# Attention and a selective scan: the projection's distance from its scan, the place of a copy, and which products GpSimd takes

## The chip, the cores and the metric

The kernel runs on one core of a Trainium2 chip. The metric is device time in microseconds (us) for one execution, the median of several runs. A difference of about 0.2% is the least that a measurement of this kernel can tell from no change.

## The reference

The input x is an fp32 image batch of 2 x 256 x 256 x 128. Two layers follow each other, each with a residual and a group norm in front. Layer 0 is attention along one image axis. Layer 1 is a state space layer, and the change is in it alone. Cut to what matters:

```python
xz = x @ in_proj_w.T                      # 128 -> 512
xi, z = split(xz, 2)                      # 256 channels each
xi = silu(depthwise_conv3x3(xi))          # along h, w
dts, Bs, Cs = split(x_proj_w @ xs)        # 8, 16 and 16 rows
delta = softplus(dt_w @ dts + dt_b)       # 256 channels
h_t = exp(delta_t * A) * h_(t-1) + (delta_t * xs_t) * B_t   # state 256 x 16
y_t = sum_n h_t[:, n] * C_t[n] + Ds * xs_t
y = layer_norm(y) * silu(z)
out = x + y @ out_proj_w.T
```

The recurrence runs over all 65536 pixels of an image in order, for 256 channels times 16 states.

## The kernel before, in words

The first part (attention, to about 2.5 ms) is not touched. The second part works in 128 *steps*: 64 per image, each of R = 4 image rows, so T = 1024 pixels.

**Units and slots.** A step's recurrence has 256 x 16 = 4096 rows, that is NU = 32 *units* of 128 partitions (32 channels times 4 states). Units are numbered t = 32 k + i for step k. In order of i they run over halves h of the channels (16 units each), in a half over four groups m of states, and in a group over four quarters q of channels. One *slot* of the schedule belongs to each unit. Each compute engine executes in the order in which the loop at the end of the kernel writes it out by hand; only the DMA queue of SyncE is ordered by the framework's scheduler.

A unit passes through these pieces:

- `decay(t)` (L956, ScalarE): exp(delta * A) of a unit into a PSUM tile da. There are two such tiles, for even and odd units, so a decay follows the last reader of the unit two before it.
- `drive(t)` (L966, GpSimd): (delta * x) * B for a *pair* of units into the SBUF tile hb, one 128 x 2048 instruction. hb has three buffers. It reads du_r and bb.
- `scan(t)` (L978, VectorE): the recurrence along T with da, hb and the state kept from the step before. It overwrites da, or, for a *pooled* unit, its half of hb.
- the product with C: `product(t)` on VectorE (L992, 128 x 1024) or, for pooled pairs, `products(t)` on GpSimd (L1001, 128 x 2048, two slots later), into yc, which has four pair buffers. Pooled pairs start at 6, 14, 22, 26 and 30 of each step: ten of the 32 products. [...]
- `remember(t)` (L983, ScalarE): the last column of the scan into the state.
- `add_up(t)` (L1024, PE): adds four units' yc into y in PSUM, six slots after the group's first unit. `start_up` (L1015) begins y with Ds * xs. `y_out` (L1037, ScalarE) copies y to SBUF seven slots after the last group's first unit, so at slots 3 and 19 of a step.

**Loads.** `fetch(t)` runs six slots ahead and loads, through SyncE's queue alone, rows of B and C repeated over partitions (bb, cc; two buffers each, L928) and delta and delta * xs (delta_r, five buffers; du_r, three pair buffers; L942). These come from DRAM tiles that the projection of the step wrote.

**Projection.** `project(k)` lays the pieces that make a step's inputs into slots relative to `base`: the image rows are turned and normalised (base, base + 1), a 3 x 3 conv as nine PE matmuls in four groups (`conv`, `conv_out`), the gate z (`gate`, `gate_out`, `silu_z` at base + 28, L718), `silu_xs` at base + 36 (L695), the rows for B, C and dt (`states`, `size`), `softplus` at base + 52 (L763) and, on GpSimd, `times`, which makes delta * xs in two halves (base + 55 and 56, L773) and writes them to DRAM. Each Silu or Softplus sits between two table loads of ScalarE. All the PE pieces share one PSUM buffer.

**Output.** `finish_row` brings one image row to the output in nine slots, starting at slots 8, 16, 24 and 32 after the end of its step: turn (PE), statistics and norm (ScalarE, L840 to L852), turn back, `gated` (VectorE, yg, L871), `mix` (PE) and `leave`.

In each slot the order was: the drive two to three units ahead, a pooled pair's products, the decay of the next unit, the scan and product of this one, the copy of y, the pieces of projection and output, the sums on PE, and the state.

Of the kernel before, what the change touches and what calls it, by code (L numbers as in the profile page):

```python
# [10 lines left out]
ALU = mybir.AluOpType  # L11
# [10 lines left out]
def attn_then_ssm_kernel(  # L22
# [26 lines left out]
    nc = tc.nc  # L49
# [78 lines left out]
    NSG = NS // SR  # L128
# [149 lines left out]
    with ExitStack() as actx:  # L278
# [242 lines left out]
        end = B * NA  # L521
        BY = 6
        with tc.manual_schedule(engines=engines):
            load(0)
            for n in range(-1, end + 1):
# [22 lines left out]
                if new:  # L548
                    project(n + 1, "m0", "qT", wqk)
# [3 lines left out]
                if new:  # L553
                    project_out(n + 1, "qT", bqk)
                    project(n + 1, "m1", "v1", wv1)
                    project_out(n + 1, "v1", bv1_c)
# [30 lines left out]
    NU = NCG * NSG  # L587
    NM = NQ * NSG

    POOLED = (6, 14, 22, 26, 30)  # L590
    s1 = ctx.enter_context(tc.tile_pool(name="s1", bufs=1))
    s2 = ctx.enter_context(tc.tile_pool(name="s2", bufs=2))
    s3 = ctx.enter_context(tc.tile_pool(name="s3", bufs=3))
# [27 lines left out]
    def project(k):  # L621

        b, s = steps[k]
        rs, sh = gn1[b]
        base = k * NU - 72
        n = min(R, H - 1 - R * s)
        v = given[k] = {}
        o = {}
# [150 lines left out]
        for r in range(0, n, RB):  # L779
            t = base + r // RB  # L780
# [3 lines left out]
        for c in range(4):  # L784
            h, i = divmod(c, NB)
            t = base + c * CY + 3
# [125 lines left out]
    def unit(t):  # L912

        k, i = divmod(t, NU)
        h, i = divmod(i, NM)
        m, q = divmod(i, NQ)
        return k, h, m, q

    spreads, repeats = {}, {}

    def fetch(t):
        k, h, m, q = unit(t)
        v = given[k]
        if q == 0:

            for name, row in (("bb", m * SR), ("cc", NS + m * SR)):
                tl = repeats[name, k, h, m] = s2.tile([P, T], F32, name=name)
                nc.sync.dma_start(  # L928
                    out=tl, in_=v["bc"][row : row + SR, :].partition_broadcast(CQ)
                )  # L930
        if m == 0:

            for name in ("delta", "du"):
                if name == "delta":
                    tl = s5.tile([P, T], F32, name="delta_r")
                elif q % 2 == 0:
                    pair = spreads["pair", k, h, q] = s3.tile([P, 2, T], F32, name="du_r")
                    tl = pair[:, 0, :]
                else:
                    tl = spreads["pair", k, h, q - 1][:, 1, :]  # L940
                spreads[name, k, h, q] = tl
                nc.sync.dma_start(  # L942
                    out=tl,
                    in_=v[name][h, q * CQ : (q + 1) * CQ, :]
                    .unsqueeze(1)
                    .to_broadcast([CQ, SR, T]),
                )

    def pooled(t):
        return t % NU - t % 2 in POOLED  # L950

    def decay(t):
        k, h, m, q = unit(t)
        da = units[t]["da"] = ps_d.tile([P, T], F32, name=f"da{t % 2}")
        g = h * NQ + q
        nc.scalar.activation(  # L956
            da, spreads["delta", k, h, q], AF.Exp, scale=a_neg[:, g, m : m + 1]
        )

    def drive(t):  # L960

        k, h, m, q = unit(t)
        hb = s3.tile([P, 2, T], F32, name="hb")
        units[t] = {"pair": hb, "hb": hb[:, 0, :]}
        units[t + 1] = {"hb": hb[:, 1, :]}
        nc.gpsimd.tensor_tensor(  # L966
            hb,
            spreads["pair", k, h, q],
            repeats["bb", k, h, m].unsqueeze(1).to_broadcast([P, 2, T]),
            ALU.mult,  # L970
        )

    def scan(t):
        k, h, m, q = unit(t)
        u = units[t]
        st = states_of[steps[k][0]][:, h * NQ + q, m : m + 1]
        u["h"] = u["hb"] if pooled(t) else u["da"]
        nc.vector.tensor_tensor_scan(u["h"], u["da"], u["hb"], st, ALU.mult, ALU.add)  # L978

    def remember(t):  # L980
        k, h, m, q = unit(t)
        st = states_of[steps[k][0]][:, h * NQ + q, m : m + 1]
        nc.scalar.copy(st, units[t]["h"][:, T - 1 : T])  # L983

    def product(t):
        k, h, m, q = unit(t)
        u = units[t]
        if t % 2 == 0:
            yc = s4.tile([P, 2, T], F32, name="yc")
            for i in range(2):  # L990
                units[t + i]["yc"] = yc[:, i, :]
        nc.vector.tensor_tensor(u["yc"], u["h"], repeats["cc", k, h, m], ALU.mult)  # L992

    def products(t):

        k, h, m, q = unit(t)
        hb = units[t]["pair"]
        yc = s4.tile([P, 2, T], F32, name="yc")
        for i in range(2):
            units[t + i]["yc"] = yc[:, i, :]  # L1000
        nc.gpsimd.tensor_tensor(  # L1001
            yc, hb, repeats["cc", k, h, m].unsqueeze(1).to_broadcast([P, 2, T]), ALU.mult
        )
# [3 lines left out]
    def start_up(t):  # L1007

        k, h, _, _ = unit(t)
        xr = s1.tile([P, T], F32, name="xr")  # L1010
        nc.sync.dma_start(out=xr, in_=given[k]["xs"][h])
        y = outs["y"] = ps_y.tile([P, T], F32, name="y")
        for i in range(NB):
            cols = slice(i * TB, (i + 1) * TB)
            nc.tensor.matmul(y[:, cols], d_diag[:, h, :], xr[:, cols], start=True, stop=False)  # L1015

    def add_up(t):

        _, _, m, _ = unit(t)
        y = outs["y"]  # L1020
        for i in range(NB):
            cols = slice(i * TB, (i + 1) * TB)
            for q in range(NQ):
                nc.tensor.matmul(  # L1024
                    y[q * CQ : (q + 1) * CQ, cols],
                    sel,
                    units[t + q]["yc"][:, cols],
                    start=False,
                    stop=(m == NSG - 1),
                )  # L1030
        for q in range(NQ):
            del units[t + q]

    def y_out(t):
        k, h, _, _ = unit(t)
        ys[k, h] = s2.tile([P, T], F32, name=f"ys{h}")
        nc.scalar.copy(ys[k, h], outs["y"])  # L1037

    for k in range(len(steps)):
        project(k)  # L1040
        finish(k)
    end = len(steps) * NU
# [7 lines left out]
    with tc.manual_schedule(engines=engines):  # L1050
        for t in range(min(slots), max(slots) + 1):
            if 0 <= t + AHEAD < end:
                fetch(t + AHEAD)
            if 0 <= t < end and t % (NU * NSTEP) == 0:
                st = s1.tile([P, NCG, NSG], F32, name="state")
                nc.gpsimd.memset(st, 0.0)
                states_of[steps[t // NU][0]] = st
            if 0 <= t + 3 < end and t % 2:
                drive(t + 3)
            if 0 <= t - 2 < end and t % 2 == 0 and pooled(t - 2):  # L1060
                products(t - 2)
            if 0 <= t + 1 < end:
                decay(t + 1)
            if 0 <= t < end:
                scan(t)
                if not pooled(t):
                    product(t)
            if 0 <= t - 7 < end and unit(t - 7)[2:] == (NSG - 1, 0):
                y_out(t - 7)
            others, on_pe = slots.pop(t, ((), ()))  # L1070
            for piece, args in others:
                piece(*args)
            for piece, args in on_pe:
                piece(*args)
            if 0 <= t - 5 < end and (t - 5) % NM == 0:
                start_up(t - 5)
            if 0 <= t - 6 < end and (t - 6) % NQ == 0:
                add_up(t - 6)
            if 0 <= t < end:
                remember(t)  # L1080


# [35 lines left out]
```

## Time and profile before

| | |
|---|---|
| median of 3 runs | 16278.99 us (16275.81 to 16286.14) |
| span of the profiled execution | 16298.5 us |
| VectorE (DVE) busy | 14642.8 us, 90% |
| PE busy | 13879.5 us, 85% |
| GpSimd (POOL) busy | 13035.7 us, 80% |
| ScalarE (ACT) busy | 10842.9 us, 67% |
| DMA | 3452 MB, 212 GB/s on the mean |
| first scan of the steps | 2678.85 us |
| drives (L966) | 2048 of 4538 ns |
| scans (L978) | 4096 of about 2340 ns |
| products on VectorE (L992) | 2816 of 1225 ns |
| products of pairs on GpSimd (L1001) | 640 of 4545 ns |

The shares of the whole span mix the attention part with the steps. In a row of a group, the first number after the bar is busy time in us, the second the mean of one instruction in ns; after the second bar stands how long the engine was idle just before these instructions, and what ended most of that idle time. In the timeline each row begins with start and duration in us.

### The profile page before, as it was taken

Reading aid. Unit: us, or ns where it says so; the run is one execution under the profiler, and the core shown is the slowest. Engines: PE = TensorE matmul, PEld = TensorE weight load, DVE = VectorE, ACT = ScalarE, POOL = GpSimd, SP = SyncE. Lnnn points to the kernel's source line nnn. Section 1 sums busy time; section 2 is a strip of 40 time slices with the busy share of each in tenths; the row PEclk is TensorE's granted clock in tenths of the full one; section 3 lists DMA queues with packets and bytes.
Section 4 is the critical chain, followed back from the end, with each engine's and each line's share of the span. In section 5 each row is a group of like instructions: output and inputs, shape, how many; then the busy total and the mean of one; then the engine's idle time right before and its main releaser. Section 6 shows DMA issues by size and latency. Waiting matters only on the chain. (4 is left out here: it accounts for less than half of the span.)

```text
span 16298.5 us, 178168 instructions
## 1 busy us (share of the span) xinstructions
PE 13879.5 (85%) x59451; PEld 7046.9 (43%) x59451; DVE 14642.8 (90%) x12484; ACT 10842.9 (67%) x20003; POOL 13035.7 (80%) x3216
## 2 busy tenths in 40 slices
PE   6999997888888888888888888888888888888886
PEld 5877783333333333333333333333333333333333
DVE  7665555999999999999999999999999999999998
ACT  3555554667666666766666666666776676677665
POOL 0111114999999999999999999999999999999998
PEclk9999998999999999999999999999999999999998
DMA  4322223666666666666666666666666666666665
GB/s 183 132 92 78 94 78 135 236 233 237 237 230 233 237 233 236 239 232 235 232 237 232 232 229 234 236 234 234 238 234 233 234 237 233 236 239 232 234 232 180
DMA packets 1428907, 3452.13 MB, mean 212 GB/s; under 512 B 119784, under 2 KB 711184, under 8 KB 1407504
## 3 DMA queue, kind: packets, MB, share of 16 engines
q1 hardware_dynamic: 1427984, 3440.73, 61.0%
q8 instruction: 468, 7.67, 0.2%
q14 instruction: 455, 3.73, 0.1%
HBM read 2752.41 MB, written 687.88 MB: 211 GB/s over the span
## 5 line engine op out<-in xcount | busy, mean ns | idle before, releaser
L966 POOL TENSOR_TENSOR hb<-du_r,bb 128x2048 f32<-128x2048 f32 x2048 | 9237.6, 4538 | 354.3 <-DVE da L978 296.2
L978 DVE TENSOR_TENSOR_SCAN da<-da,state,hb 128x1024 f32<-128x1024 f32 x2816 | 6607.2, 2346 | 163.1 <-ACT da L956 160.2
L676 PE MATMUL u_ps<-xn,w_tap 128*128 128x512 f32 x9216 | 4481.8, 629 | 617.0 <-ACT state L983 607.5
L956 ACT ACTIVATE da<-delta_r,a_neg 128x1024 f32<-128x1024 f32 x4096 | 4588.5, 1120 | 91.8 <-ACT state L983 0.4
L992 DVE TENSOR_TENSOR yc<-da,cc 128x1024 f32<-128x1024 f32 x2816 | 3449.1, 1225 | 287.3 <-PE y L1024 113.8
L1001 POOL TENSOR_TENSOR yc<-hb,cc 128x2048 f32<-128x2048 f32 x640 | 2908.7, 4545 | 527.6 <-ACT state L983 493.0
L978 DVE TENSOR_TENSOR_SCAN hb<-da,state,hb 128x1024 f32<-128x1024 f32 x1280 | 2941.9, 2336 | 199.1 <-ACT state L983 166.4
L676 PEld LDWEIGHTS u_ps<-xn,w_tap 128*128 128x128 f32 x9216 | 1762.1, 201 | 3108.4 <-issue 2110.6
L1024 PE MATMUL y<-yc,sel 128*32 128x512 f32 x16384 | 2409.3, 712 | 16.6 <-POOL yc L1001 16.6
L435 POOL TENSOR_TENSOR x1g<-xc,bo_all 128x512 f32<-128x512 f32 x256 | 315.7, 1271 | 1844.3 <-DVE stats L484 1843.1
L983 ACT COPY state<-da 128x1 f32<-128x1 f32 x2816 | 458.2, 163 | 1266.7 <-DVE yc L992 1262.4
L828 PE MATMUL yt<-centre,ys 128*128 128x256 f32 x4096 | 1029.7, 395 | 250.2 <-ACT ob L889 250.2
L1024 PEld LDWEIGHTS y<-yc,sel 128*32 128x32 f32 x16384 | 477.4, 121 | 1743.3 <-issue 1518.6
L702 PE MATMUL z_ps<-xn,w_z 128*128 128x512 f32 x1024 | 691.8, 763 | 628.2 <-ACT sz L713 389.6
L385 ACT ACTIVATE e<-s_ps,nmx 128x256 f32<-128x256 f32 x1024 | 479.4, 478 | 967.9 <-DVE nmx L376 956.7
L983 ACT COPY state<-hb 128x1 f32<-128x1 f32 x1280 | 247.0, 193 | 1262.2 <-DVE hb L978 1262.2
L828 PEld LDWEIGHTS yt<-centre,ys 128*128 128x128 f32 x4096 | 741.3, 191 | 430.1 <-ACT ob L889 347.8
L744 PE MATMUL dt_ps<-xd,w_dt 8*128 8x512 f32 x1024 | 611.7, 678 | 345.2 <-ACT state L983 193.7
L889 ACT COPY ob<-o_ps 128x256 f32<-128x256 f32 x512 | 191.0, 373 | 948.6 <-PE o_ps L879 948.0
L879 PE MATMUL o_ps<-w_out,szr 128*128 128x128 f32 x4096 | 799.2, 277 | 0.0
L879 PE MATMUL o_ps<-w_out,yg 128*128 128x128 f32 x4096 | 797.9, 277 | 0.0
L352 DVE TENSOR_TENSOR v<-v_ps,bv_all 128x512 f32<-128x512 f32 x256 | 177.1, 692 | 594.5 <-PE v_ps L345 594.5
(133 smaller groups left out, 17404.3 us busy)
## 6 DMA issues: line engine op xcount, KB each, us to landing
bb<-bc_d SPq DMA_DIRECT2D x1024, 512.0 KB, 4.2
cc<-bc_d SPq DMA_DIRECT2D x1024, 512.0 KB, 4.8
delta_r<-delta_d SPq DMA_DIRECT2D x1024, 512.0 KB, 6.6
du_r<-du_d SPq DMA_DIRECT2D x1024, 512.0 KB, 5.5
sz_d<-sz SPq DMA_DIRECT2D x128, 1024.0 KB, 6.6
szr<-sz_d SPq DMA_DIRECT2D x512, 256.0 KB, 4.1
xs_d<-xs SPq DMA_DIRECT2D x128, 1024.0 KB, 9.0
xr<-xs_d SPq DMA_DIRECT2D x256, 512.0 KB, 5.7
```

Source lines behind the costliest of these rows:

```text
L676: nc.tensor.matmul(o["u"], w_tap[:, h, tap, :], xn[:, i * RB + dy : i * RB + dy + RB, dx : dx + W], start=(tap == 0), stop=(tap == 8),)
L702: nc.tensor.matmul(o["z"], w_z[:, h, :], xn[:, 1 + i * RB : 1 + (i + 1) * RB, 1 : W + 1], start=True, stop=True,)
L744: nc.tensor.matmul(o["dt"], w_dt[:, h, :], o["xd"][0:DR, i * TB : (i + 1) * TB], start=True, stop=True,)
L828: nc.tensor.matmul(o["yt"][:, j, :], ys[k, h][:, t0 + j * P : t0 + (j + 1) * P], centre[:, (1 - h) * P : (1 - h) * P + DI], start=(h == 0) ...
L879: nc.tensor.matmul(o["o"][:, j, :], o[by][:, h, j * P : (j + 1) * P], w_out[:, i, h, :], start=False, stop=(j == WT - 1 and h == NH - 1 an ...
L956: nc.scalar.activation(da, spreads["delta", k, h, q], AF.Exp, scale=a_neg[:, g, m : m + 1])
L966: nc.gpsimd.tensor_tensor(hb, spreads["pair", k, h, q], repeats["bb", k, h, m].unsqueeze(1).to_broadcast([P, 2, T]), ALU.mult,)
L978: nc.vector.tensor_tensor_scan(u["h"], u["da"], u["hb"], st, ALU.mult, ALU.add)
L983: nc.scalar.copy(st, units[t]["h"][:, T - 1 : T])
L992: nc.vector.tensor_tensor(u["yc"], u["h"], repeats["cc", k, h, m], ALU.mult)
L1001: nc.gpsimd.tensor_tensor(yc, hb, repeats["cc", k, h, m].unsqueeze(1).to_broadcast([P, 2, T]), ALU.mult)
L1024: nc.tensor.matmul(y[q * CQ : (q + 1) * CQ, cols], sel, units[t + q]["yc"][:, cols], start=False, stop=(m == NSG - 1),)
```

## The change

It has three parts. The projection of a step begins 64 slots, two whole steps, ahead of the step's first scan instead of 72, so each of its pieces moves by eight slots against the scans. The copy of y comes at the end of its slot, after the pieces and the state, so that ScalarE has done the slot's other work before it stands for the sums. And GpSimd takes eleven products of a step: the pair at 10 in place of the pair at 26, and one single product, that of unit 13, issued on GpSimd in the next slot before the decay.

```diff
-    POOLED = (6, 14, 22, 26, 30)
+    POOLED = (6, 10, 14, 22, 30)
+    SINGLE = 13
...
-        base = k * NU - 72
+        base = (k - 2) * NU
...
-        return t % NU - t % 2 in POOLED
+        return t % NU - t % 2 in POOLED or t % NU == SINGLE
...
-        nc.vector.tensor_tensor(u["yc"], u["h"], repeats["cc", k, h, m], ALU.mult)
+        eng = nc.gpsimd if pooled(t) else nc.vector
+        eng.tensor_tensor(u["yc"], u["h"], repeats["cc", k, h, m], ALU.mult)
...
             if 0 <= t - 2 < end and t % 2 == 0 and pooled(t - 2):
                 products(t - 2)
+            if 0 <= t - 1 < end and (t - 1) % NU == SINGLE:
+                product(t - 1)
...
-            if 0 <= t - 7 < end and unit(t - 7)[2:] == (NSG - 1, 0):
-                y_out(t - 7)
             others, on_pe = slots.pop(t, ((), ()))
...
             if 0 <= t < end:
                 remember(t)
+            if 0 <= t - 7 < end and unit(t - 7)[2:] == (NSG - 1, 0):
+                y_out(t - 7)
```

## The prediction, made before the changed kernel was run

> **What bounds the kernel now.** I read the page's busy shares first, then the busy time of each engine in the long stretch of steps (3000 to 16200 us), then the groups of that stretch by shape, and last the timeline of one step (the one whose first scan starts at 9031.5 us).
>
> ```profile
> 3000.00:16200.00 13200.00, 11117.48 (x44672) 4983.83 (x44670) 12694.85 (x7226) 9157.44 (x15911) 12372.31 (x2868) 0.93 0.68 234
> ```
>
> The columns are PE, PEld, DVE, ACT, POOL, then clock, DMA share, GB/s. VectorE is busy 96% of the stretch, GpSimd 94%; nothing else is close.
>
> ```profile
> L966 POOL TENSOR_TENSOR hb<-du_r,bb 128x2048 f32<-128x2048 f32 x1993 | 8989.4, 4538 | 317.6 <-DVE da L978 278.6
> L978 DVE TENSOR_TENSOR_SCAN da<-da,state,hb 128x1024 f32<-128x1024 f32 x2742 | 6433.6, 2346 | 28.5 <-ACT da L956 25.6 <-POOL state L1056 2.9
> ...
> L992 DVE TENSOR_TENSOR yc<-da,cc 128x1024 f32<-128x1024 f32 x2742 | 3358.4, 1225 | 278.8 <-PE y L1024 109.6 <-DVE da L978 2.7 <-issue 2.2
> L978 DVE TENSOR_TENSOR_SCAN hb<-da,state,hb 128x1024 f32<-128x1024 f32 x1244 | 2859.1, 2336 | 192.9 <-ACT state L983 160.9 <-ACT da L956 27.0
> L1001 POOL TENSOR_TENSOR yc<-hb,cc 128x2048 f32<-128x2048 f32 x623 | 2831.6, 4545 | 507.8 <-ACT state L983 480.2 <-issue 12.2 <-PE u_ps L676 8.8
> ...
> L773 POOL TENSOR_TENSOR xs<-delta,xs 128x1024 f32<-128x1024 f32 x248 | 587.4, 2369 | 0.0
> ```
>
> The last column is the one to read. No scan ever waits for a drive (L966): VectorE waits for ScalarE (its decays) and a little for PE. GpSimd waits for VectorE, so it runs ahead and has slack. From the first scan (2678.85) to the last (about 16239) 128 steps pass, so a step takes 105.9 us; that is the sum of VectorE's own work, about 103.0, and some 2.9 of waits.
>
> ```profile
> 9098.56 1.01 ACT L1037 COPY ys<-y 128x1024 f32<-128x1024 f32 x1 [2.11 <-PE y L1024]
> 9099.47 0.85 ACT L852 ACTIVATE yn<-yt,rstd 128x256 f32<-128x256 f32 x2
> ...
> 9100.89 1.12 ACT L956 ACTIVATE da<-delta_r,a_neg 128x1024 f32<-128x1024 f32 x1
> 9102.02 1.28 ACT L718 ACT_TABLE_LOAD   x1
> 9103.32 1.91 ACT L718 ACTIVATE sz<-sz 128x2048 f32<-128x2048 f32 x1
> 9105.25 1.28 ACT L619 ACT_TABLE_LOAD   x1
> ...
> 9106.73 1.12 ACT L956 ACTIVATE da<-delta_r,a_neg 128x1024 f32<-128x1024 f32 x1
> ...
> 9107.96 4.59 DVE L978 TENSOR_TENSOR_SCAN hb<-da,state,hb 128x1024 f32<-128x1024 f32 x2 [1.44 <-ACT state L983]
> ```
>
> This is where the largest of those waits is made. ScalarE stands 2.11 us at the copy of y, which is ahead of slot 19's other pieces; a Silu between two table loads follows, and scan 22, which comes early because no product of VectorE's stands before it, waits 1.44 us.
>
> **What the Trainium skill says.** "GPSIMD Engine Reference", section 3.1, gives 4497 ns for a GpSimd tensor_tensor on 2048 fp32 against 2293 ns on VectorE; this trace agrees (4538 and 4545 ns; VectorE 1225 ns at 1024). So a moved product takes about twice as long. "ScalarE: Activation LUTs", "What ACT_TABLE_LOAD costs", gives 1283 ns for a load and a drain on top; the load agrees, but no drain is seen between the lines above, so I count load, Silu, load as 4.5 us. "DMA: Bandwidth & Descriptors", "Anatomy of one DMA", says that a semaphore wait "happens on the issuing sequencer before dispatch". All loads here are issued by SyncE, so one waiting load holds all behind it; the trace agrees (SyncE issues nothing for up to 9 us, then several at once).
>
> **The change part by part.** Offsets come from the timeline: a scan with its product takes 3.58 us (even slots) or 3.52 (odd), a scan whose product is GpSimd's 2.25, each yg 0.60; on GpSimd a drive takes 4.49, a pair's product 4.55, a 1024 product 2.33 (from L773).
>
> *Eleven products instead of ten.* VectorE loses one product: 21 x 3.55 + 11 x 2.25 + 4 x 0.60 = 101.7 us a step (before: 22 and 10, 103.0). GpSimd gains 2.33: 16 x 4.49 + 5 x 4.55 + 3 x 2.33 = 101.6. Both engines now have the same work, so each wait of one for the other counts.
>
> *Copy of y at the end of its slot.* It removes no work. In slot 19 ScalarE no longer stands before the norm, the copy behind it and the state; the copy waits where scan 19's product is awaited anyway. At slot 3 it now stands in front of decay 5.
>
> *Projection 64 ahead.* All projection pieces move by 8 of 32 slots. As rows of the output recur every 8 slots, what shares a slot with them hardly changes: the three Silu and Softplus groups still stand two slots before a pooled pair (now slots 4, 20, 28). But delta x xs (L773) moves to slots 23 and 24, so the first du_r of the next step can be read only late in the step. In the built program SyncE's queue runs: write of du, delta_r 32, du_r 32, delta_r 33, cc, du_r 33, delta_r 34, du_r 34, write of sz, delta_r 35, du_r 35. delta_r 35 waits for the decay of scan 30 to free its buffer, which stands behind silu_z on ScalarE; queued behind it is du_r 35, and drive 34 waits for that. That is a new wait.
>
> Loop A, counted from scan 20: VectorE to the end of product 27, 3.58 + 4.12 + 4.50 + 14.20 = 26.4; decay 29 begins 0.25 later; from there to the end of decay 30 is 6.96 (9100.89 to 9107.85 above); delta_r is issued, 0.7; du_r is issued at 34.4 and lands L later. Then GpSimd without a pause from drive 34 to drive 20 of the next step: ten drives 44.9, four pairs' products 18.2, one single 2.33, together 65.4. Wakes 0.2. Sum: 100.0 + L. For L:
>
> ```profile
> delta_r<-delta_d SPq DMA_DIRECT2D x1024, 512.0 KB, 6.6
> du_r<-du_d SPq DMA_DIRECT2D x1024, 512.0 KB, 5.5
> ```
>
> (issues, size, median us to landing) and, of the tile du_r alone, the spread:
>
> ```profile
> DMA to landing us min/median/max: 3.3/5.5/9.2
> ```
>
> A du_r that is second in an otherwise quiet queue lands in 4.7 to 5.0 (the one of 9123.9 lands after 4.7); third or fourth in a train it takes 6.7. Here only sz (1 MB, issued 3 us earlier, 4.0 alone) and delta_r are ahead. I take 4.9: 104.9 us.
>
> Loop B, counted from the product of pair 6: GpSimd to the end of drive 28: nine drives 40.4, four pairs 18.2, three singles 7.0, together 65.6; scan 28 waits for that; VectorE from scan 28 to the end of scan 7: 12.2 + 26.5 = 38.7; wakes 0.3. In it ScalarE makes scan 6 wait: decay 5 begins 1.3 after scan 4 (state, copy of y), its Silu group ends decay 6 6.96 later, at 8.3, and scan 6 could begin at 7.7: 0.6. Sum: 105.2.
>
> The step is the longer loop, 105.2, and 0.1 for what the two do to each other: 105.3 against 105.9. That is 0.64 x 128 = 82 us less. PE's later start of a conv and the residue of ScalarE's work lie beside VectorE.
>
> *Start.* The first scan stood at its decay, which ScalarE reaches after the last conv, the turn of the third projection and silu_xs:
>
> ```profile
> 2678.85 2.36 DVE L978 TENSOR_TENSOR_SCAN da<-da,state,hb 128x1024 f32<-128x1024 f32 x1 [133.74 <-ACT da L956]
> ```
>
> With 8 slots fewer in front these come after it. The first drive (2658.7) then sets it: 2663.3, and the decay after silu_z at about the same time, so near 2665: 14 us less. The tail is untouched. 16279 - 82 - 14 = 16183 us.
>
> **The rivals.** *The late du_r (slower).* If the transfers bunch up and L is 6.7, loop A takes 106.7: 16279 + 0.8 x 128 - 14 = 16367. For it: the queue has three waits in a row, and landings go to 9.2. Against: the trains of today come from loads that all waited for one event. *VectorE sets it (faster still).* If GpSimd's waits fall into one another (L 4.4, no wait at scan 6), loops of 104.4 remain: 16279 - 192 - 14 = 16073. Against: both loops would have to be lucky. *No change.* GpSimd has no slack left, so waits of scans 16, 20 and 28 for drives take the place of waits for ScalarE: a step of 105.9, 16265. For it: idle GpSimd of 6.6 us a step today would have to fall below 4.3 for any gain.
>
> **How the numbers follow.** Forecast 0.50, late du_r 0.22, no change 0.15, VectorE alone 0.13. The range reaches from the fast rival to the slow one, 16065 to 16370. Of the forecast's half nearly all is faster by over 0.2% (below 16246), with the fast rival 0.62; within 0.2% 0.15; slower 0.23.
>
> **What would show it.** Right: a step of 105.3; scans 20 and 28 wait for POOL hb; drive 34 waits for the DMA of du_r for some 2 to 3 us; scan 22 no longer waits; a POOL group of 128 products of 1024 at about 2.37 us; the first scan near 2665. Wrong: waits of drives for du_r over 5 us a step (the late du_r), or no scan waiting for a drive (VectorE alone), or a new wait of decays on the copy of y.

## The result, and the profile after

The changed kernel takes 16677.32 us (median of 4 runs, 16672.46 to 16680.63) against 16278.85 us before: a ratio of 1.0244, 95% interval 1.0226 to 1.0262. It is 2.4% slower; 16183 us was forecast, and the range ended at 16370.

From the first scan to the last, 128 steps now take 13942.2 us, 108.95 each, where they took 105.96. That is 2.99 x 128 = 383 us more; the first scan comes 9 us earlier (2669.61 against 2678.85), the profiled spans differ by 372 (16670.4 against 16298.5, which is 20 above before's median), so all of the loss is in the steps.

The groups by shape of the changed kernel over the steps, 3000 to 16200 us (after the second bar: idle time just before these instructions, and who ended it):

```profile
L968 POOL TENSOR_TENSOR hb<-du_r,bb 128x2048 f32<-128x2048 f32 x1938 | 8766.6, 4549 | 889.4 <-DMA du_r<-du_d 702.6 <-DVE yc L995 79.2 <-DVE yg L873 54.3
L980 DVE TENSOR_TENSOR_SCAN da<-da,state,hb 128x1024 f32<-128x1024 f32 x2543 | 5971.8, 2348 | 818.3 <-POOL hb L968 779.3 <-ACT ys L1040 14.3 <-ACT da L958 12.8
...
L980 DVE TENSOR_TENSOR_SCAN hb<-da,state,hb 128x1024 f32<-128x1024 f32 x1331 | 3055.1, 2333 | 1.6 <-ACT state L985 1.6
L1004 POOL TENSOR_TENSOR yc<-hb,cc 128x2048 f32<-128x2048 f32 x606 | 2744.6, 4529 | 3.9 <-ACT state L985 3.9
...
L995 POOL TENSOR_TENSOR yc<-hb,cc 128x1024 f32<-128x1024 f32 x121 | 285.7, 2361 | 0.0
```

Read it against the same rows of before. There the drives waited for VectorE and no scan waited for a drive. Now the drives wait 702.6 us for the DMA of du_r, a wait that the old list doesn't have, and the scans wait 779.3 us for drives. The pooled scans, which waited 160.9 us for ScalarE's state, wait 1.6. The single product is there, at 2361 ns.

Busy time over 3000 to 15800 us, before and then after (PE, PEld, DVE, ACT, POOL, clock, DMA share, GB/s):

```profile
3000.00:15800.00 12800.00, 10822.69 (x43451) 4847.11 (x43450) 12306.62 (x7005) 8904.09 (x15453) 11994.95 (x2781) 0.93 0.68 234
```

```profile
3000.00:15800.00 12800.00, 10812.73 (x42269) 4788.32 (x42268) 11839.86 (x6691) 8650.96 (x15024) 11935.98 (x2822) 0.90 0.65 228
```

Multiplied by the step and divided by 12800, VectorE's work falls from 101.9 to 100.8 us a step and GpSimd's rises from 99.3 to 101.6, as intended. But VectorE now stands idle 8.2 us of a step (4.1 before) and GpSimd 7.4 (6.7 before). Two in-order engines with almost equal work, both idle: something between them closes a loop longer than either.

The timeline of SyncE's queue in the changed kernel, at the end of step 60 (start, duration):

```profile
9295.70 0.42 SPq L776 DMA_DIRECT2D du_d<-xs  x1
9296.17 0.52 SPq L944 DMA_DIRECT2D delta_r<-delta_d  x1
9296.74 2.71 SPq L944 DMA_DIRECT2D du_r<-du_d  x1
9299.54 0.55 SPq L944 DMA_DIRECT2D delta_r<-delta_d  x1
9300.19 0.55 SPq L930 DMA_DIRECT2D cc<-bc_d  x1
9300.79 0.59 SPq L944 DMA_DIRECT2D du_r<-du_d  x1
9301.47 0.68 SPq L944 DMA_DIRECT2D delta_r<-delta_d  x1
9302.24 1.37 SPq L944 DMA_DIRECT2D du_r<-du_d  x1
9304.14 0.37 SPq L723 DMA_DIRECT2D sz_d<-sz  x1
9306.76 0.51 SPq L944 DMA_DIRECT2D delta_r<-delta_d  x1
9307.33 0.64 SPq L944 DMA_DIRECT2D du_r<-du_d  x1
```

and GpSimd's timeline in the same place:

```profile
9295.55 9.07 POOL L968 TENSOR_TENSOR hb<-du_r,bb 128x2048 f32<-128x2048 f32 x2
9309.46 4.54 POOL L968 TENSOR_TENSOR hb<-du_r,bb 128x2048 f32<-128x2048 f32 x1 [4.84 <-DMA du_r<-du_d]
9317.53 4.52 POOL L968 TENSOR_TENSOR hb<-du_r,bb 128x2048 f32<-128x2048 f32 x1 [3.53 <-DMA du_r<-du_d]
```

The order in the queue is the predicted one: after the write of du come four delta_r, four du_r, one cc and the write of sz, and the last du_r is the one that drive 34 (9317.53) waits for. It was issued at 9307.33 and landed at 9317.31, after 9.98 us. The busy times of that stretch, and of the 9.98 us from the issue of the last du_r to its landing:

```profile
9295.00:9317.00 22.00, 20.81 (x86) 9.36 (x86) 19.55 (x12) 14.63 (x21) 14.16 (x4) 0.86 0.99 370
```

```profile
9307.33:9317.31 9.98, 8.48 (x51) 5.06 (x49) 8.29 (x6) 5.09 (x9) 4.54 (x1) 1.00 1.01 394
```

The DMA engines are busy 99% of the time and move 370 GB/s, in the last part all of the time and 394, where the mean over before's steps is 234: the train is limited by its bytes. Its landings follow one another by 1.3 to 1.6 us for 0.5 MB (9303.57, 9304.83, 9306.4, 9307.66). Over 108 steps the last du_r is issued 34.3 us after scan 20 and lands after 8.5 us (median), up to 10.0.

### The profile page after: what moved, and what is told of

Its sections match the earlier page's. It is cut to its first block, busy times and chain, and to the rows that moved or that the text cites. A ratio compares the mean times of both kernels' runs of the same rounds, so it can differ in the third digit from the quotient of the medians.

```text
span 16670.4 us, 178654 instructions
## 1 busy us (share of the span) xinstructions
PE 14173.4 (85%) x59451; PEld 7123.2 (43%) x59451; DVE 14510.4 (87%) x12356; ACT 10829.0 (65%) x20003; POOL 13332.6 (80%) x3344
## 5 line engine op out<-in xcount | busy, mean ns | idle before, releaser
L980 DVE TENSOR_TENSOR_SCAN da<-da,state,hb 128x1024 f32<-128x1024 f32 x2688 | 6312.2, 2348 | 979.8 <-POOL hb L968 813.9
L678 PE MATMUL u_ps<-xn,w_tap 128*128 128x512 f32 x9216 | 4296.7, 607 | 7.1 <-ACT sz L715 4.0
L995 DVE TENSOR_TENSOR yc<-da,cc 128x1024 f32<-128x1024 f32 x2688 | 3291.8, 1225 | 181.1 <-PE y L1027 4.6
L980 DVE TENSOR_TENSOR_SCAN hb<-da,state,hb 128x1024 f32<-128x1024 f32 x1408 | 3231.7, 2333 | 2.4 <-ACT state L985 2.4
L678 PEld LDWEIGHTS u_ps<-xn,w_tap 128*128 128x128 f32 x9216 | 1704.4, 194 | 2437.5 <-issue 1781.0
L1027 PE MATMUL y<-yc,sel 128*32 128x512 f32 x16384 | 2662.7, 756 | 31.5 <-POOL yc L1004 31.5
L704 PE MATMUL z_ps<-xn,w_z 128*128 128x512 f32 x1024 | 771.7, 844 | 746.8 <-ACT sz L715 433.9
L1027 PEld LDWEIGHTS y<-yc,sel 128*32 128x32 f32 x16384 | 551.8, 127 | 1994.5 <-issue 1648.1
L746 PE MATMUL dt_ps<-xd,w_dt 8*128 8x512 f32 x1024 | 733.4, 802 | 514.9 <-ACT delta L757 350.5
L775 POOL TENSOR_TENSOR xs<-delta,xs 128x1024 f32<-128x1024 f32 x256 | 606.4, 2369 | 97.3 <-ACT delta L765 97.3
```

What stands on the lines that cost most here:

```text
L678: nc.tensor.matmul(o["u"], w_tap[:, h, tap, :], xn[:, i * RB + dy : i * RB + dy + RB, dx : dx + W], start=(tap == 0), stop=(tap == 8),)
L704: nc.tensor.matmul(o["z"], w_z[:, h, :], xn[:, 1 + i * RB : 1 + (i + 1) * RB, 1 : W + 1], start=True, stop=True,)
L746: nc.tensor.matmul(o["dt"], w_dt[:, h, :], o["xd"][0:DR, i * TB : (i + 1) * TB], start=True, stop=True,)
L995: eng.tensor_tensor(u["yc"], u["h"], repeats["cc", k, h, m], ALU.mult)
L1027: nc.tensor.matmul(y[q * CQ : (q + 1) * CQ, cols], sel, units[t + q]["yc"][:, cols], start=False, stop=(m == NSG - 1),)
```

## The experiments

Theory A: the late du_r, by way of SyncE's queue, closes the loop. Rivals: B, the eleven products stand in the wrong place on GpSimd; C, the late copy of y makes scans 2 and 4 wait. Each ratio is against the kernel before (16285.3 to 16285.5 us in these runs).

**The change with the projection 72 ahead again.**

```diff
-        base = (k - 2) * NU
+        base = k * NU - 72
```

> The changed kernel with the projection back at 72 slots ahead; the eleven products and the late copy of y stay. Theory A (late du_r: the rows for drive 34 are read behind silu_z's tail in SyncE's queue and land some 10 us later): with the projection eight slots earlier these rows are there long before, no drive waits for a DMA, a step falls from 109.0 to 105.5 us or less and the time to 16100 to 16250 us. Theory B (GpSimd overload: eleven products leave it no slack, whoever feeds it): the step stays above 107.5 us, over 16500 us.

Measured 16649.9 us, 1.0223 (1.0208 to 1.0239). Its list of waits (total us, times, longest), 3000 to 15800 us:

```profile
DVE da L980 <- POOL hb L968: 614.5, 118, 5.7
...
POOL yc L1004 <- ACT state L985: 431.6, 227, 2.2
```

No drive waits for a DMA, and yet a step takes 108.7 us: one scan a step (118 waits in 118 steps, 5.2 us each), scan 20, waits for its drive. With 72 slots the two halves of delta x xs stand at slots 15 and 16. Between the products of pair 6 and the end of drive 20 GpSimd then has products 6, 10, 14 and 13, both halves and the drives between: 43.3 us without a pause. VectorE needs 65.1 from scan 20 to the end of scan 7 of the next step, on which the products of pair 6 wait (the second line names ScalarE, because the copy of scan 7's state ends last, 0.2 us after the scan). The sum, 108.4 and 0.3 of wakes, is the step. So B holds for *this* kernel, and undoing one part of the change does not show what the part costs in the whole.

**The move of the projection alone**, on the kernel before.

```diff
-        base = k * NU - 72
+        base = (k - 2) * NU
```

> The kernel before with the projection at 64 slots alone; ten products and the old place of the copy. Theory A: the late rows alone cost, so a step takes 109 us or more, 16650 to 16800 us, with drive 34 waiting for du_r and scan 36 waiting for its drive. Theory B: GpSimd has its slack back and hides the late rows, 16250 to 16320 us.

Measured 17686.25 us, 1.0860 (1.0841 to 1.0878); a step of 117.0 us. Its list of waits:

```profile
DVE da L978 <- POOL hb L966: 967.9, 295, 7.5
...
POOL hb L966 <- DMA du_r<-du_d: 620.9, 69, 10.4
```

Scan 2 waits 6.4 us for its drive and scan 4 1.8. In the built program the cc load of the next step waits for the products of pair 26 and stands in SyncE's queue ahead of du_r's: in step 60 SyncE issues nothing from 27.2 to 35.8 us after scan 20, when these products end, and the last du_r is issued at 38.9 and lands at 49.3. Behind drive 34 scan 2 begins at 54.0, and from there VectorE needs 62.7 to scan 20 (medians): together 116.7, the step. The move alone costs 1401 us, and it is the late du_r that sets the step. The waits are those of theory A, but the time is 886 us above A's range; neither theory had the held queue in it.

**The change with the ten old products.**

```diff
-    POOLED = (6, 10, 14, 22, 30)
-    SINGLE = 13
+    POOLED = (6, 14, 22, 26, 30)
+    SINGLE = -1
```

> The changed kernel with the ten products of before; projection at 64 and the copy at the end of its slot stay. Theory A: as slow as the changed kernel or slower, 16600 to 16750 us, since VectorE has one product more and the rows come as late. Theory B: below 16350 us.

Measured 17546.23 us, 1.0775 (1.0759 to 1.0791); a step of 115.9. Its list of waits:

```profile
DVE da L980 <- POOL hb L968: 1106.2, 319, 8.4
...
POOL hb L968 <- DMA du_r<-du_d: 632.1, 126, 7.2
```

Scan 0 now waits 6.4 us for its drive, scans 2 and 4 some 2 each. The time is 796 us above A's range; here too SyncE's queue is held until the products of pair 26 end (34.3 us after scan 20 in step 60), scan 2 begins at 53.8, and 61.9 later comes scan 20: 115.7 in sum. The eleven products of the change are therefore worth 869 us beside the move (17546 to 16677): with pair 26 no longer GpSimd's, the queue is not held so long. B falls as a cause of the loss in the whole change.

**The change with the copy of y in its old place.**

```diff
+            if 0 <= t - 7 < end and unit(t - 7)[2:] == (NSG - 1, 0):
+                y_out(t - 7)
             others, on_pe = slots.pop(t, ((), ()))
...
-            if 0 <= t - 7 < end and unit(t - 7)[2:] == (NSG - 1, 0):
-                y_out(t - 7)
```

> The changed kernel with the copy of y back in front of the pieces of its slot; projection at 64 and eleven products stay. Theory A: within 50 us of the changed kernel's 16677 us. Theory C (the copy at the end of slot 3 stands before decay 5 and makes the new waits of scans 2 and 4): the waits of scans 2 and 4, 2.7 us a step together, vanish, and the time falls below 16400 us.

Measured 16744.88 us, 1.0281 (1.0266 to 1.0296), 68 us more than the change. Its list of waits:

```profile
POOL hb L968 <- DMA du_r<-du_d: 786.2, 195, 8.6
...
DVE da L980 <- POOL hb L968: 548.2, 371, 3.0
...
DVE hb L980 <- ACT state L985: 132.9, 124, 1.5
```

Scan 22 waits 1.1 us for its state again (the third line), and scans 2 and 4 still wait 1.0 and 1.9 for their drives. C falls; A's margin of 50 us was missed by 18.

**The change with du_r asked for before delta_r.**

```diff
-            for name in ("delta", "du"):
+            for name in ("du", "delta"):
```

> The changed kernel, but fetch asks for du ahead of delta, so that in SyncE's queue the last du_r stands before the delta_r that waits for a decay behind silu_z; the write of sz still stands before it. Theory A (a step is about 100 us plus the time L from the issue of the last du_r to its landing, counted from its present place): it is issued some 2.5 us earlier with about the same L, so a step falls from 109.0 to 106.5 us, 16300 to 16450 us. Theory D (the products crowded ahead of scan 20 set the step, as they do with the projection at 72): within 60 us of 16677 us.

Measured 16531.01 us, 1.0152 (1.0137 to 1.0167), 81 us above A's range. Its list of waits:

```profile
DVE da L980 <- POOL hb L968: 626.7, 496, 2.0
...
POOL hb L968 <- DMA du_r<-du_d: 567.7, 184, 6.3
```

Both waits are there still. The last du_r is issued 31.5 us after scan 20 instead of 34.3, but takes 10.2 to land instead of 8.5: of 2.8 us won at the issue only 1.1 reach the landing, and the step falls by about 1.1, to 107.85. D falls (146 us less than the changed kernel), and of A the part "about the same L". The order within this train helps little.

**The same, with the store of sz asked for five slots later**, out of the train.

```diff
+        def store_z():
             v["sz"] = dr.tile([NH, P, T], F32, name="sz_d")
...
         at(base + 28, silu_z)
+        at(base + 33, store_z)
```

> As the one with du ahead of delta, and besides the write of sz to DRAM is asked for five slots after silu_z, so that no load of du waits behind silu_z any more. Theory A: the last du_r is issued 5 us earlier than in the changed kernel, drive 34 waits for it by under 2.5 us, and the loop through pair 6's product sets the step at 105 to 106 us: 16130 to 16300 us. Theory D: above 16600 us.

Measured 16278.39 us, 0.9997 (0.9989 to 1.0006): the whole loss is gone. Its list of waits:

```profile
DVE da L983 <- POOL hb L971: 340.4, 361, 1.7
...
POOL hb L971 <- DMA du_r<-du_d: 295.1, 206, 2.9
```

The last du_r now lands 29.1 + 9.5 = 38.6 us after scan 20. From drive 34 to the end of drive 20 GpSimd takes 65.8, wakes 0.3. So loop A is 42.8 + 66.1 = 108.9 in the change (step 108.95), 41.7 + 66.1 = 107.8 with du_r first (107.85), and 104.7 here, where the step is 105.97. Theory A gives the steps of the first two from their landings; in the third its loop is no longer the longest: the products of pair 6 now wait 1.1 us, most of it for scan 7 and the copy of its state, so loop B sets the step. Measured on this trace, B is 65.9 (GpSimd from these products to the end of drive 28) + 39.8 (VectorE from scan 28 to the end of scan 7) + 0.2 = 105.9.

**The copy of y alone**, on the kernel before.

```diff
-            if 0 <= t - 7 < end and unit(t - 7)[2:] == (NSG - 1, 0):
-                y_out(t - 7)
             others, on_pe = slots.pop(t, ((), ()))
...
                 remember(t)
+            if 0 <= t - 7 < end and unit(t - 7)[2:] == (NSG - 1, 0):
+                y_out(t - 7)
```

> The kernel before with the copy of y at the end of its slot alone; projection at 72 and ten products. My reading: the wait of scan 22 (1.1 us a step) and of scan 21 (0.2) go, 104.7 us a step, 16100 to 16180 us. Rival: other waits take their place, 16250 to 16300 us.

Measured 16184.53 us, 0.9940 (0.9925 to 0.9955), just above the range expected. The copy alone makes the kernel 101 us faster. Two lines of its list of waits, 3000 to 15800 us:

```profile
DVE yc L992 <- PE y L1024: 144.0, 121, 2.2
...
DVE hb L978 <- ACT state L983: 103.1, 121, 1.6
```

The pooled scans wait 103.1 us for ScalarE's state, 157.7 before in the same stretch; what remains is scan 22, 0.8 us a step. In exchange the product of unit 28 waits 1.2 us for PE, more than before in sum (144.0 against 107.5 us). The first gives 0.5 us of a step. The scans' waits for decays fall too, from 52.2 to 13.5 us in sum, which about makes up for the product's wait. The step falls by 0.8; what gives the rest is not shown.

**The eleven products alone**, that is the changed kernel with 72 slots and the old place of the copy.

```diff
-        base = (k - 2) * NU
+        base = k * NU - 72
...
+            if 0 <= t - 7 < end and unit(t - 7)[2:] == (NSG - 1, 0):
+                y_out(t - 7)
             others, on_pe = slots.pop(t, ((), ()))
...
                 remember(t)
-            if 0 <= t - 7 < end and unit(t - 7)[2:] == (NSG - 1, 0):
-                y_out(t - 7)
```

> The kernel before with the eleven products of the change alone; projection at 72 and the copy of y in its old place. Theory D: 43.2 us of GpSimd from pair 6's products to the end of drive 20 and 65.0 of VectorE, 108.5 us a step, as in the run with only the projection taken back: 16600 to 16720 us, with scan 20 waiting over 4 us. Rival (the copy at its new place had a share in that run's loss): below 16550 us.

Measured 16706.8 us, 1.0258 (1.0243 to 1.0273). Scan 20 waits 3.0 us, less than the 4 expected, product 12 1.9, product 8 1.0, and the step is 109.3. Beside the early halves of delta x xs the eleven products cost 421 us with the copy in its old place, and 465 with it in its new one (16184.53 to 16649.9).

**Ten products, but pair 10 in place of pair 26**, 72 slots, late copy.

```diff
-    SINGLE = 13
+    SINGLE = -1
...
-        base = (k - 2) * NU
+        base = k * NU - 72
```

> Projection at 72, copy of y at the end of its slot, ten products with the pair at 10 in place of the pair at 26 and no single one. It has as many products as the run with the late copy alone (16185 us) and differs in their place. Theory D (place): from pair 6's products to the end of drive 20 GpSimd now has 40.9 us of work, VectorE from scan 20 to the end of scan 7 has 65.0, so a step is 106.2 us or a little more, 16270 to 16400 us, and scan 20 waits for its drive. Theory B (number): 16160 to 16210 us.

Measured 16342.21 us, 1.0036 (1.0022 to 1.0050), a step of about 106.3; scan 20 waits 1.9 us. The same count as in the kernel with the late copy alone is 158 us slower: it is the place of a product that costs, not the number.

**An eleventh product where GpSimd used to stand idle**: 72 slots, late copy, the old five pairs and unit 3.

```diff
-    POOLED = (6, 10, 14, 22, 30)
-    SINGLE = 13
+    POOLED = (6, 14, 22, 26, 30)
+    SINGLE = 3
...
-        base = (k - 2) * NU
+        base = k * NU - 72
```

> Projection at 72, copy of y at the end of its slot, the pairs 6, 14, 22, 26 and 30 of before, and as the eleventh product that of unit 3 alone, in a stretch where GpSimd waits for VectorE in the kernel before. Theory D (what counts is where GpSimd's products stand against its drives and times, not their number): VectorE's work falls by 1.26 us a step with no new wait for a drive, 103.5 to 104.2 us a step, 15940 to 16050 us. Theory B (eleven are too many anywhere): over 16300 us.

Measured 15903.95 us, 0.9768 (0.9753 to 0.9782), 36 us below D's range and faster than both kernels. Its groups by shape, 3000 to 15800 us:

```profile
L968 POOL TENSOR_TENSOR hb<-du_r,bb 128x2048 f32<-128x2048 f32 x1991 | 8990.6, 4545 | 52.0 <-DVE da L980 3.5
L980 DVE TENSOR_TENSOR_SCAN da<-da,state,hb 128x1024 f32<-128x1024 f32 x2611 | 6120.8, 2344 | 5.0 <-POOL state L1059 3.6 <-ACT da L958 1.4
...
L980 DVE TENSOR_TENSOR_SCAN hb<-da,state,hb 128x1024 f32<-128x1024 f32 x1368 | 3141.7, 2335 | 70.0 <-ACT state L985 55.9 <-ACT da L958 12.5 <-POOL hb L968 1.1
...
L995 POOL TENSOR_TENSOR yc<-hb,cc 128x1024 f32<-128x1024 f32 x125 | 295.2, 2361 | 0.0
```

```profile
3000.00:15800.00 12800.00, 11048.86 (x44606) 4933.70 (x44605) 12488.72 (x7089) 9136.76 (x15878) 12639.30 (x2989) 0.92 0.71 241
```

The scans wait 75.0 us in all, 1.1 of it for drives, the drives 52.0, and VectorE and GpSimd are busy 97.6% and 98.7%. Here both have nearly equal work, and no loop between them is much longer: the step, 102.95 us, is 1.3 above GpSimd's own work.

## Why the prediction was wrong

By its own steps:

- **Work of the engines.** Right: 1.3 us less on VectorE was forecast, 1.1 measured (101.9 to 100.8 busy; the prediction's 103.0 and 101.7 count from begin to begin, short pauses included); GpSimd 101.6, as forecast.
- **Copy of y.** Right: scan 22 no longer waits. Alone it is worth 101 us, though scan 22 still waits 0.8 us there; in the whole change 68.
- **Start.** 14 us forecast, 9 measured.
- **Loop A, issue.** Right: delta_r 35 and du_r 35 behind silu_z, issued 34.3 us after scan 20 (34.4 forecast).
- **Loop A, GpSimd.** 65.4 forecast, 65.8 measured, because each drive directly behind a product begins 0.08 us late, some five times.
- **Loop A, L. This is the step that failed.** "Here only sz (1 MB, issued 3 us earlier, 4.0 alone) and delta_r are ahead. I take 4.9". L was 8.5. The prediction had just listed the queue, nine transfers before these, and then counted only those issued in the last 3 us. But a transfer issued earlier still takes the engines' time as long as it has not landed. When the last du_r is issued, six transfers with itself are on their way (median of 102 steps): three du_r, two delta_r and sz, 3.7 MB, where the prediction counted three of them, 2.1 MB. The 1.6 MB left out take 4.2 us at the 370 GB/s of that stretch; L was 3.6 us longer than taken.

  An estimate of this kind was possible beforehand, but not from the ten transfers of the train alone: from 9296.17 to 9307.33 eight delta_r and du_r, a cc of 0.52 MB and sz of 1.05 are issued, 5.8 MB, which would be through at 9311.8, only 4.5 us after the last issue. The five issued just ahead (cc, three small transfers of output rows and the write of du, 1.6 MB) were still on their way too; with them it is 7.3 MB, 19.8 us, and the end at 9316.0. The last landed at 9317.3. "DMA: Bandwidth & Descriptors", "Where 436 GB/s comes from", gives about 358 GB/s as what the HBM side allows between HBM and SBUF. The trace exceeds it (394 GB/s in the last 9.98 us), so here it is no limit; but an estimate from that page, 20.5 us for the 7.3 MB, would have put L in this step at 9.3, so for the rate no trace of after was needed.

  Loop A came out 4.0 us above its 104.9 (L 3.6, GpSimd 0.4), and so passed loop B. L's 3.6 us x 128 = 461 us is the bulk of the error of 494.
- **Loop B.** 105.2 forecast, 106.0 measured where it set the step (the store of sz late): the same late begins of drives (0.3), and VectorE's part 39.8 instead of 38.7 + 0.6. Even there, with the loads in time, the change brings nothing (16278.39 us).
- **The signs named.** Scans 20 and 28 wait for drives (1.7 and 0.6 us), but so do 4, 16 and 2 (1.9, 1.4, 0.8); the drives wait 674.8 us for du_r over 117.5 steps, 5.7 us each, above the 5 that the prediction named as the sign of the late du_r.
- **The rivals.** "The late du_r" was what happened, with its mechanism right and its L, 6.7, still too small. It was held down because "the trains of today come from loads that all waited for one event". The same is true of the new train: its ten transfers stand in SyncE's queue behind the write of du, issued at 9295.70, when GpSimd had just made the second half of delta x xs (9295.62).

The shares of the parts do not add up: copy alone -101 us, products alone +421, move alone +1401, sum +1721, all three together +398. The eleven products clash with delta x xs at slots 15 and 16 and go with it at 23 and 24; the move makes du_r late, and taking pair 26 away makes it less late. What stays open: the late store of sz was run only with du_r asked for first, so its own share isn't known; loads on a second queue weren't tried.

## What to carry to other kernels

When a change makes a group of loads wait for one event, price the last of them by all bytes that will not have landed when it is issued, over the rate that the DMA engines reach when full, not by the landing of a lone transfer. On two in-order engines with nearly equal work, count the loops between them (which instruction waits for which, what stands between, until the first comes round again) before moving an instruction: a product in a gap of GpSimd brought 281 us over the late copy alone, and pair 10 in place of pair 26 lost 158. And undo a part of a change in both directions, alone and from the whole, since parts that share a loop do not add.

## What the runs showed of the hardware

Asking for a transfer 2.8 us earlier within a full train brought its landing forward by only 1.1 us (L from 8.5 to 10.2). In the changed kernel's step, the four du_r of the second half of the channels, outside that train, landed after 4.0 to 5.3 us (medians). Over one profile the landings of this tile spread threefold, 3.4 to 10.7 us with a median of 6.3, and the median that the page prints says nothing of the one transfer that matters.
